# Statistics in a reading of their own, transposes and layer norm in one stage, variances of four chunks side by side

## The chip, the cores and the metric

The kernel runs on one NeuronCore of a Trainium2 chip. Its engines are TensorE (PE, with its weight loads PEld), VectorE (DVE), ScalarE (ACT), GpSimd (POOL) and SyncE (SP); they run from queues of their own and meet through semaphores. SP, ACT and POOL issue DMA transfers, which share 16 DMA engines. The metric is the device time of one execution in microseconds (us). The kernel before takes 5235.69 us, the median of three runs (5234.29 to 5239.15).

## The reference

An image `x` of 256 x 256 pixels and 128 channels goes through four residual layers, each behind a group normalisation `_gn` over 32 groups of 4 channels and all pixels. All is float32. Only the head of layer 0 is touched by the change:

```python
def _gn(v, G=32, eps=1e-5):
    g = v.reshape(B_, H_, W_, G, C_ // G)
    m = mean(g, axis=(1, 2, 4)); s = var(g, axis=(1, 2, 4))
    return ((g - m) / sqrt(s + eps)).reshape(v.shape)
# layer 0: z = _gn(x)
mu = mean(z, -1); var = mean(square(z - mu), -1)
zn = (z - mu) * rsqrt(var + EPS) * ln_scale + ln_bias   # layer norm over the channels
q, k, v, g = zn @ Wq, zn @ Wk, zn @ Wv, sigmoid(zn @ Wg) # four heads of 32
scores = q k^T / sqrt(32) + (zn @ Wb)                    # attention along rows, with a pair bias
x = x + ((g * softmax(scores) v) @ Wo)
```

Layer 1 is a recurrence in the frequency plane, whose small 7 x 7 kernels are Fourier transformed first (the "spectrum"); layer 2 is a triangle product, layer 3 a 3 x 3 convolution with a dense layer. Each takes `x` from the layer before.

## The kernel before, in words

The kernel keeps every image transposed in DRAM: channels on the 128 partitions, 65536 pixels along the free dimension (`xT`, `x1T` ..., `znT` for the normalised one). `run` (L1343) calls one function after another. What concerns us is what comes ahead of the attention loop.

*`attention_weights` (L218) and `bounded` (L380 and on)* load layer 0's weights over ACT's queue, scale them, and compute from small Gram matrices a bound on the scores, whose flag decides later which attention loop runs. `wv`, `wq` and so on are scaled on DVE (L237); `terms` takes one square root on ACT.

*`transpose_in` (L158)* goes over 64 blocks of 1024 pixels. SP loads a block `xin` (512 KB); PE transposes it in eight 128 x 128 pieces into `pt` (L202); DVE copies one half to `xo` and ACT the other (L208, L206), so that eight neighbouring pixels stand together; DVE takes two `bn_stats` per block (L211) for the group statistics; POOL stores `xT` (L212). There are five buffers of each tile and three of `pt`. Between blocks 12 and 57, sixteen calls of `spectrum` (L181) each do eight small matmuls `ph` and a copy to `H` on ACT (L188); after eight of them ACT gathers `H` into `HH` by four copies over 14 partitions (L192), and SP stores it to DRAM. The statistics are merged by `group_affine` (L75), with matmuls `pm`, `pv` over groups and a square root `sd` on ACT; `centering` (L122) makes a matrix `lc` that scales and subtracts the channel mean in one matmul, and a column `cb` (matmul `pc`).

*The first part of `attention` (L293 to L372)* goes over the same 64 blocks again. SP loads pairs of blocks back from `xT` (1 MB, L311). Per block: `centre`, two matmuls `zc` of 512 pixels; `squares`, ACT's square `sq` and DVE's copy with the column added, `zs`; `normalise`, two matmuls `var` of the squares with a matrix of 1/128, so that every partition holds the variance, ACT's Ln and Exp for the inverse root `rs`, DVE's product `zn`, and POOL's scale and bias (L336). Per pair, `pair_bias`: four matmuls `pbias` of 32 output rows, each in a column strip of its own, a copy `bi`, POOL's store of `znT` (L346) and four small stores of the bias by SP (L349). This part is written in program order on each engine (`keep_in_program_order`, L299); elsewhere a scheduler orders the instructions of each engine when the kernel is built. At the end the bias is loaded back (L288), and the attention loop begins with `ppq`.

Pools of tiles have a fixed number of buffers; a tile's producer waits until the tile that had the buffer is released. PSUM has eight banks of 512 float32 per partition.

## Time and profile before

| what | before |
|---|---|
| median of three runs | 5235.69 us |
| the profiled execution | 5238.88 us |
| its span on the chip | 5237.0 us |
| mean granted TensorE clock | 0.975 |
| PE, DVE, ACT, POOL busy | 4997.8, 4091.4, 3684.9, 344.4 us |
| transposing stage (to the last `pc`) | 0 to 227.3 us |
| layer norm stage (first `zc` to last `pbias`) | 227.5 to 493.8 us |
| DMA, whole span | 788.58 MB, mean 151 GB/s |

A line of a group reads: line of the kernel, engine, operation, output<-input by the program's names, shapes, count; then busy us and mean ns of one; then idle time of the engine ahead of these, and what ended it. One float32 matmul appears as two records, each of a weight load and a product. A line of a stretch gives its length, and the busy us of PE, weight loads, DVE, ACT, POOL with their instruction counts, then the granted clock (1.00 is full), the share of the DMA engines, and GB/s. A line of the timeline or of the chain gives the start in us and the duration, merged over neighbours. In waits, "a <- b: 65.9, 30, 11.8" means that a waited for b 65.9 us in 30 times, 11.8 at the longest.

### The profile page before, as it was taken

What the parts mean: (1) busy time and instruction counts of PE and PEld (TensorE: products, weight loads), DVE (VectorE), ACT (ScalarE), POOL (GpSimd) and SP (SyncE); (2) the same over time, 40 slices, a digit from 0 to 9 for tenths busy, and PEclk for the clock granted to TensorE, in tenths of its full rate; (3) what the DMA queues carried; (4) which work ended last, traced back from release to release, by engine and by line L of the source; (5) the groups of instructions that cost most, each with busy time, mean ns of one, the idle gap of its engine ahead of it and who ended that gap; (6) DMA issues with size and microseconds to landing.
All of it is one profiled execution on the core that took longest, in us unless ns stands there. A gap on an engine that the chain in (4) does not pass through costs nothing.

```text
span 5237.0 us, 75959 instructions
## 1 busy us (share of the span) xinstructions
PE 4997.8 (95%) x30067; PEld 2805.6 (54%) x30067; DVE 4091.4 (78%) x4886; ACT 3684.9 (70%) x5051; POOL 344.4 (7%) x552
## 2 busy tenths in 40 slices
PE   6699999999999899999999998999999989989999
PEld 4433555555555333333333333349999944339999
DVE  5665999999999799999999999554433446679886
ACT  4376888888888799999999998883333357762110
POOL 1132000000000000000000000000011000000000
PEclk7799999999999899999999999999999999999999
DMA  8875222222222122122222221767766678855432
GB/s 290 335 271 206 73 86 82 85 80 83 86 85 82 62 70 70 66 73 68 70 70 67 73 70 65 286 253 272 251 229 231 224 288 295 295 206 188 148 123 65
DMA packets 185921, 788.58 MB, mean 151 GB/s; under 512 B 36083, under 2 KB 39432, under 8 KB 136384
## 3 DMA queue, kind: packets, MB, share of 16 engines
q1 hardware_dynamic: 120212, 514.73, 29.2%
q0 software_dynamic: 60416, 268.46, 13.3%
q8 instruction: 240, 3.93, 0.3%
q10 hardware_dynamic: 4936, 0.50, 0.1%
q14 instruction: 117, 0.96, 0.1%
HBM read 512.28 MB, written 271.32 MB: 150 GB/s over the span
## 4 chain that ended last, share of the span: by engine, by line
issue 50%; PE 41%; DVE 5%; POOL 2%; DMA 1%; ACT 1%; POOLq 0%; ACTq 0%; DVEq 0%; SPq 0%
PE z L60 9%; PE m L60 7%; PE zc L60 4%; PE po L60 4%; PE nd L60 3%; PE sc L60 3%; PE var L60 2%; PE py L60 2%; DVE stats L966 1%; DVE x L966 1%; PE ppq L60 1%; PE ppv L60 1%; PE px L60 1%; PE ppk L60 1%; PE ppg L60 1%
## 5 line engine op out<-in xcount | busy, mean ns | idle before, releaser
L471 DVE TENSOR_TENSOR e<-sc,bT 128x1024 f32<-128x1024 f32 x512 | 602.9, 1219 | 52.0 <-PE sc L60 52.0
L54 ACT ACTIVATE e<-e 128x1024 f32<-128x1024 f32 x512 | 540.3, 1055 | 64.1 <-DVE e L471 54.9
L966 DVE TENSOR_TENSOR LR<-z,sg 128x512 f32<-128x512 f32 x256 | 268.3, 1049 | 365.6 <-ACT sg L54 358.6
L60 PE MATMUL m<-U,v 128*128 128x128 f32 x4608 | 516.6, 276 | 6.6 <-DVE v L1281 6.6
L60 PEld LDWEIGHTS m<-U,v 128*128 128x128 f32 x4608 | 516.4, 192 | 6.7 <-DVE v L1281 6.7
L60 PE MATMUL z<-wf,zt 128*128 128x128 f32 x4096 | 460.9, 276 | 4.3 <-DVE zn L966 3.6
L60 PEld LDWEIGHTS z<-wf,zt 128*128 128x128 f32 x4096 | 460.6, 193 | 5.5 <-DVE zn L966 4.4
L54 ACT ACTIVATE sg<-z 128x512 f32<-128x512 f32 x256 | 152.8, 597 | 308.7 <-PE z L60 306.8
L60 PE MATMUL var<-sq,omat 128*128 128x512 f32 x768 | 360.8, 599 | 1.2 <-ACT rs L54 1.2
L54 ACT ACTIVATE rs<-var,eps 128x1024 f32<-128x1024 f32 x192 | 213.2, 1111 | 169.7 <-PE var L60 169.7
L60 PE MATMUL sc<-tq,tk 32*128 32x256 f32 x4096 | 299.0, 403 | 2.3 <-DVE e L471 1.4
L471 DVE TENSOR_TENSOR ks<-e 128x1024 f32<-128x1024 f32 x256 | 300.6, 1215 | 0.0
L60 PEld LDWEIGHTS sc<-tq,tk 32*128 32x128 f32 x4096 | 187.6, 185 | 160.3 <-issue 97.1
L60 PE MATMUL nd<-e,tv 128*32 128x256 f32 x4096 | 271.8, 383 | 0.0
L60 PE MATMUL zc<-xin,lc 128*128 128x512 f32 x512 | 248.6, 609 | 6.0 <-DVE zn L966 5.5
L54 ACT ACTIVATE dn<-dn 128x512 f32<-128x512 f32 x384 | 241.6, 629 | 12.7 <-DVE dn L471 1.9
L60 PEld LDWEIGHTS var<-sq,omat 128*128 128x128 f32 x768 | 137.9, 189 | 203.8 <-issue 155.2
L60 PE MATMUL av<-y,ident 128*128 128x512 f32 x384 | 192.2, 609 | 44.0 <-DVE y L803 44.0
L60 PE MATMUL po<-LR 128*128 128x256 f32 x1024 | 222.2, 380 | 6.9 <-DVE LR L966 6.9
L1318 ACT COPY m4s<-m 128x512 f32<-128x512 f32 x32 | 18.7, 585 | 286.8 <-PE m L60 286.8
L60 PEld LDWEIGHTS po<-LR 128*128 128x128 f32 x1024 | 194.1, 190 | 34.2 <-DVE LR L966 7.7
L54 ACT ACTIVATE rs<-rs 128x1024 f32<-128x1024 f32 x192 | 202.9, 1057 | 6.1
(325 smaller groups left out, 10085.5 us busy)
## 6 DMA issues: line engine op xcount, KB each, us to landing
zt<-znT SPq DMA_DIRECT2D x128, 1024.0 KB
znT<-zn POOLq DMA_DIRECT2D x64, 1024.0 KB, 4.7
xin<-x2T SPq DMA_DIRECT2D x64, 1024.0 KB
xr<-x3T SPq DMA_DIRECT2D x46, 768.0 KB
xin<-in_x_dram SPq DMA_DIRECT2D x64, 512.0 KB
xT<-xo POOLq DMA_DIRECT2D x64, 512.0 KB, 10.5
xr<-xT SPq DMA_DIRECT2D x64, 512.0 KB
xin<-xT SPq DMA_DIRECT2D x32, 1024.0 KB
```

Source lines behind the costliest of these rows:

```text
L54: return self.nc.scalar.activation(out, in_, func, bias=bias, scale=scale, **kw)
L60: return self.nc.tensor.matmul(out, lhsT, rhs, start=start, stop=stop)
L471: pin = lambda f: lambda *a, **k: tc.keep_in_program_order(f(*a, **k))
L966: pin = lambda f: lambda *a, **k: tc.keep_in_program_order(f(*a, **k))
L1318: nc.scalar.copy(m4, m[4])
```

## The change

The statistics get a reading of `x` of their own, and the transposes move into the layer norm stage.

- `statistics` replaces `transpose_in`. It reads `x` untransposed in 32 tiles `xin` of 2048 pixels (pixels on partitions), subtracts the first pixel from all (`sh`, `xs` on DVE), squares on ACT (`sqx`), and lets PE sum both over the partitions into one PSUM bank, `acc`: four column strips of 32 rows, two for the sums and two for the squares. Four matmuls with `sel` and a few DVE operations turn it into mean and variance per channel. Three tiles stay in SBUF (`kept`), so the next stage need not load them. The statistics no longer come from `bn_stats`.
- The spectrum moves with it (`kernel_rows`). `HH` is gathered in two halves, the first by ACT, the second by POOL, and stored in four pieces rather than two. `attention_weights` becomes a generator: loads first, its arithmetic at tile 23 of the program; the built order of each engine spreads both between the tiles.
- The layer norm stage goes over 32 pairs of blocks. Each round does `turn` for the next pair (16 transposes, four half copies, one `xT` store of 1 MB by POOL, one load of `xin` by SP two pairs ahead), then `variance`, one `centre`, `normalise`, `pair_bias` of the pair before, and the other `centre`. `zc` now reads `xo` in SBUF; `xT` is not read here.
- The variances of the four chunks of a pair go to four column strips of one PSUM bank (`var`, 32 rows each), so Ln and Exp run once over 512 columns rather than twice over 1024. Four row-strip matmuls with `spread` (32 rows by 128 columns of 1/32) then spread the inverse roots over all partitions, `pr`, and DVE's product reads `pr` from PSUM.
- PSUM in this stage: three buffers of two banks shared by `pt`, `zc`, `pr`, and two of one bank shared by `var` and `pbias`. The weights of the later layers are loaded in the layer norm stage; before, their loads stood among the first transposes.

```diff
+    def kernel_rows(self, sp, ps, HD_):
...
+        def spectrum(g):
+            n, g0 = divmod(2 * g, CG)
+            ph = ps.tile([P, 2, N], F32, name="ph", bufs=2)
...
+            nc.scalar.copy(H[n][:, :, g0:g0 + 2].rearrange("q u c -> q c u"), ph)
+            if g0 + 2 == CG:
+                for h in range(2):
+                    o = slice(64 * n + 32 * h, 64 * n + 32 * h + 2 * KS)
+                    u = slice(h * N // 2, (h + 1) * N // 2)
+                    for k in range(4):
+                        copy = nc.gpsimd.tensor_copy if h else nc.scalar.copy
+                        copy(HH[o, :, CG * k:CG * (k + 1)], H[n][32 * k:32 * k + 2 * KS, u])
+                    nc.sync.dma_start(HD_[n][:, u], HH[o])
+    def statistics(self, wp, weights, HD_, kept, src):
...
+            io = c.enter_context(self.pool(name="p0", bufs=2))
...
+            acc = ps.tile([P, 512], F32, name="acc")
+            order = list(range(KEPT, NM)) + list(range(KEPT))
+            for n, m in enumerate(order):
+                if m < KEPT:
+                    xin = kept[m]
+                else:
+                    xin = io.tile([P, 2, 1024], F32, name="xin", bufs=3)
+                nc.sync.dma_start(xin, src(m))
+                for b in range(2):
+                    xs = io.tile([P, 1024], F32, name="xs")
+                    V.tensor_tensor(xs.rearrange("p (t c) -> p t c", t=8), xin[:, b].rearrange("p (t c) -> p t c", t=8),
+                                    sh.unsqueeze(1).to_broadcast([P, 8, P]), ALU.subtract)
+                    sq = io.tile([P, 1024], F32, name="sqx")
+                    self.act(sq, xs, AF.Square)
+                    for j, t in enumerate((xs, sq)):
+                        for h in range(2):
+                            o = 64 * j + 32 * h
+                            self.mm(acc[o:o + 32], ones[:, :32], t[:, h * 512:(h + 1) * 512],
+                                    start=n == 0 and b == 0, stop=n == NM - 1 and b == 1)
+                if n == 2:
+                    spectrum = self.kernel_rows(sp, ps, HD_)
+                    next(weights)
+                elif 5 <= n < 21:
+                    spectrum(n - 5)
+                elif n == 23:
+                    weights = next(weights)
...
-                def normalise(b):
-                    var = ps.tile([P, 2, 512], F32, name="var", bufs=1)
-                    for k in range(2):
-                        mm(var[:, k], self.omat, sq[b][:, k * 512:(k + 1) * 512])
...
+            wide = lambda name: ps.tile([P, 1024], F32, name=name, tag="w")
+            row = lambda name: ps.tile([P, 512], F32, name=name, tag="r", bufs=2)
+            def turn(m):
+                load(m + 2)
+                xo[m] = io.tile([P, 2, P, 8], F32, name="xo")
+                for b in range(2):
+                    pt = wide("pt").rearrange("c (t p) -> c t p", t=8)
+                    for t in range(8):
+                        transpose(pt[:, t], xin[m][:, b, t * P:(t + 1) * P], self.ident)
+                    for h, f in enumerate((acopy, copy)):
+                        f(xo[m][:, b, :, 4 * h:4 * h + 4], pt[:, 4 * h:4 * h + 4].rearrange("c t p -> c p t"))
+                nc.gpsimd.dma_start(xT[:, m * 2048:(m + 1) * 2048], xo[m].rearrange("c b p t -> c (b p t)"))
...
+            def variance(m):
+                var = row("var")
+                for k in range(4):
+                    mm(var[32 * k:32 * k + 32], m32, sq[m, k // 2][:, (k % 2) * 512:(k % 2 + 1) * 512])
+                rs[m] = work.tile([P, 512], F32, name="rs")
+                act(rs[m], var, AF.Ln, bias=self.eps)
+                act(rs[m], rs[m], AF.Exp, scale=-0.5)
+            def normalise(m):
+                zn[m] = io.tile([P, 2048], F32, name="zn")
+                pr = [wide("pr") for _ in range(2)]
+                for k in range(4):
+                    mm(pr[k // 2][:, (k % 2) * 512:(k % 2 + 1) * 512], spread[32 * k:32 * k + 32], rs[m][32 * k:32 * k + 32])
+                for b in range(2):
+                    z = zn[m][:, b * 1024:(b + 1) * 1024]
+                    tt(z, zs[m, b], pr[b], ALU.mult)
                     nc.gpsimd.tensor_scalar(z, z, lns, lnb, ALU.mult, ALU.add)
...
+            turn(0)
+            centre(0, 0)
+            centre(0, 1)
+            for m in range(NM):
+                turn(m + 1)
+                variance(m)
+                centre(m + 1, 0)
+                normalise(m)
+                pair_bias(m - 1)
+                centre(m + 1, 1)
```

## The prediction

> **What bounds the kernel now.** I read the busy time by stretches first, then the rate of the DMA engines, the waits, and the chain that ended last. In the stretches (length, then busy us of PE, weight loads, DVE, ACT, POOL, then granted clock, DMA share, GB/s) two stages lie before the attention loop:
>
> ```profile
> 100.00:150.00 50.00, 27.97 (x156) 23.65 (x147) 28.82 (x48) 26.10 (x23) 8.56 (x17) 0.67 0.85 332
> 150.00:200.00 50.00, 27.64 (x138) 23.86 (x136) 30.55 (x50) 9.37 (x16) 9.01 (x17) 0.61 1.01 367
> 300.00:350.00 50.00, 50.00 (x155) 18.88 (x153) 33.20 (x32) 39.68 (x39) 18.88 (x20) 1.00 0.70 270
> 600.00:650.00 50.00, 50.00 (x523) 26.43 (x519) 46.19 (x54) 43.39 (x64) 1.60 (x3) 1.00 0.30 96
> ```
>
> Up to 227 us (transposes) no compute engine is near full and DMA is. From 227 to 494 us (layer norm) PE is full at full clock and DMA has 30% to spare. From 494 us on is attention, where PE is full again. The transposing stage in finer steps (GB/s of 40 steps between 120 and 215 us), and its waits (total us, times, longest):
>
> ```profile
> GB/s 254 376 350 369 386 421 417 417 423 416 423 411 417 421 423 417 419 669 159 78 105 205 404 367 378 385 378 400 409 416 419 416 417 419 414 421 426 424 428 426
> ```
> ```profile
> PEld pt L202 <- ACT xo L206: 65.9, 30, 11.8
> DVE xo L208 <- DMA xT<-xo: 46.2, 19, 10.9
> ```
>
> The plateau is about 420 GB/s, with a hole near 163 us where ACT copies HH (before that, four such copies held ACT from 103.3 to 117.8). So stage one is 64 MB at 420 GB/s, 160 us, and some 65 us of start, holes and tail. In the layer norm the chain returns to the same instruction every 8.06 us (start, duration):
>
> ```profile
> 374.42 1.91 PE var L60 x4
> 382.48 1.92 PE var L60 x4
> 390.54 1.91 PE var L60 x4
> ```
>
> 8.06 us is one pair of blocks, 2048 pixels, and PE has no gap in it: stage two is 32 x 8.06 = 258 us and 8 of ends.
>
> **What the Trainium skill says.** "TensorE: Matmul & The Clock Gate", Part 3: small matmuls in different 32-row or 32-column strips run at once, four row strips at N=512 measured 3.07 times faster. The trace agrees: pbias, four matmuls in column strips, takes 1.06 us below, against 4 x 0.86. The same page, Part 1 and Part 4: an idle PE falls to half clock, and transposes do not count as busy in the same way. Agrees: 0.61 to 0.67 in the transposing stage, 1.00 in the layer norm. "HBM Reference", Specifications: a core streaming alone gets about 425 GB/s; here 417 to 428. "SBUF — State Buffer", Who interferes with whom: a DVE instruction with two SBUF inputs and a GpSimd one that reads SBUF exclude each other. No row before shows such a collision.
>
> **The change, part by part.** Prices, from groups (busy us, mean ns) and, last, from the timeline (start, duration):
>
> ```profile
> L208 DVE COPY xo<-pt 128x512 f32<-128x512 f32 x64 | 43.0, 683 | 51.6 <-DMA xT<-xo 46.2 <-PE pt L202 4.8
> L206 ACT COPY xo<-pt 128x512 f32<-128x512 f32 x64 | 36.7, 588 | 108.9 <-DVE xo L208 96.8 <-DMA ev<-in_c_cols_dram 12.0
> L192 ACT COPY HH<-H 14x4096 f32<-14x4096 f32 x8 | 28.8, 3604 | 0.2
> L188 ACT COPY H<-ph 128x512 f32<-128x512 f32 x16 | 16.2, 1034 | 17.1 <-PE ph L60 17.1
> ```
> ```profile
> 402.07 1.88 PE L60 MATMUL var<-sq,omat 128*128 128x512 f32 x4
> 405.60 1.06 PE L60 MATMUL pbias<-zn,wb 128*32 128x512 f32 x8
> 504.88 1.91 PE L600 MATMUL pbt<-ident,bias 128*128 128x128 f32 x16
> 602.99 1.15 PE L60 MATMUL sc<-tq,tk 32*128 32x256 f32 x16
> ```
>
> *Removed:* the 32 MB reading of xT back, the bn_stats (78.5 us of DVE), stage one as it stood. All of 0 to 227.3 us falls away, and stage two's 266.2 us (first zc 227.5, last pbias 493.8).
>
> *Stage S (statistics).* It reads 33.6 MB: 80 us at 420 GB/s, 1.25 us per half tile (1024 pixels, 64 of them). DVE: 64 subtractions at 1.22 (row zn<-zs,rs) = 78 us, and some 45 small operations of the bound at about 0.22 = 10. ACT: 64 squares at 1.06 (row e<-e, 1055 ns, the same shape between SBUF tiles) = 68. H copies 16 x 1.03 = 16.5, HH copies 8 at half of 3.6 = 14.4, table loads and seven late DMA issues (0.45 each) = 6: 105 us. PE: per half tile four matmuls in four column strips, 0.9 to 1.1 us at full clock when the two pairs overlap as pbias does, 1.75 when they do not or the clock is half. 58 to 112, and the spectrum matmuls 15 (24.6 at the old clock).
>
> No engine alone sets S; the order in the built program does. The spectra and HH copies stand among the first 24 squares. ACT up to there: 24 x 1.06 + 16.5 + 14.4 + 1.5 + 3.2 = 61 us. Xs and its squares have two buffers each, so while ACT does six H and four HH copies in a row (13.4 us), DVE stands still and then, after three tiles (7.5 us), so do SP's loads. I add 6 us of waits: DVE's wv stands in front of the subtractions and waits for rawv, which ACT now loads only after its sixth square (a load takes some 4 us, as at the start of the old stage), and PE's queue holds spectra between the sums. The other 40 half tiles run at the DVE's and DMA's 1.25: 50 us. The first square starts at about 12.3 (row load, its broadcast, first subtraction; the old first transpose was at 16.8). The tail is acc 1.75 cold, its copy 0.7, the sums over partitions 3, and the old chain pm to pc 3.3 (224.0 to 227.3): 9. Together 12.3 + 61 + 6 + 50 + 9 = 138.
>
> Not shown before: HH's eight copies on POOL. Nearest row: its 2048-element memset, 1.79 us. Less than nothing is excluded, as the half that they take off ACT is already counted. Bounds: 0 if DVE stands still then anyway, 8 x 2.2 = 18 if each one locks the subtractions out (both inputs lie in SBUF); I take 4, as half of them fall into ACT's burst. S ends at 142, bounds 118 to 165.
>
> SP's own queue: the four HD stores wait there on POOL and ACT in front of the next tile loads. Hidden while three tiles are in hand; that is the same stall, not counted twice. Two store instructions more, 0.4 us each.
>
> *Stage B (transposes and layer norm), PE per 2048 pixels:* 16 transposes 1.91 (row pbt, same form at full clock), four zc 3.44 (as now: two take 1.72), var in column strips 1.1, pr in row strips 1.1 (row sc: 16 records of 256 columns, 1.15 overlapping the next, next start 1.08 later), pbias 1.1: 8.65. Switching between strip forms costs about 0.05 each; today pbias adds 1.18 to 6.88. I take 8.8, bounds 8.4 and 9.6.
>
> Who else: ACT 2 x 0.59 + 2 x 1.10 + 0.60 + 0.63 = 4.6 (6.5 now); DVE 2 x 0.68 + 2 x 1.28 + 2 x 1.22 + 0.68 = 7.0; POOL 2 x 1.19 + two issues 1.1 = 3.5; DMA 3.18 MB at 420 GB/s = 7.6. PE sets the pace, the cover of DMA is 1.2 us. Chains: PE queues var after 1.9 us of transposes, which covers the last square (1.1); zc (1.72) covers Ln and Exp (1.3 with handing over); xo's copies end about 0.7 before zc needs them, since DVE first finishes zs. The three wide PSUM buffers return in that order without a wait. If these covers fail, each costs its overlap, some 0.5 per round, 16 us.
>
> Ends: first transposes cold 3.6, two blocks' zc cold 6.5 (227.54 to 234.00 now), 31 rounds x 8.8 = 273, then var, Ln, Exp, pr, two products, POOL's pass: 7.5 to the last pbias. 290.6 against 266.2: +24.
>
> *Moved, at nothing:* the late weights (1.2 MB, 3 us of DMA) lie beside the first rounds, whose first three tiles are kept in SBUF and need no load; without that cover 3 us. The xT store moves behind the zn passes on POOL, which is idle 60% of a round. From the last normalise on, each engine's order is the same as before, so attention and all after cost what they cost.
>
> *Sum:* (142 - 227.3) + 24 = -61 to -62. Against the profiled execution's own 5238.88 us (span 5237.0 and 1.9 around it) that is 5177; that execution lies 3.2 us above the median of the runs, 5235.69, so 5174.
>
> **Rivals.**
> 1. *S runs at the DMA's pace* (H and HH copies fully hidden): 12 + 80 + 17 of waits and tail = S ends near 118, 5150. For it: nothing but ACT stands over 90 us. Against: two buffers only.
> 2. *S is bound by cold PE*: 64 x 1.75 + 29 = 141, in part overlapped, S ends near 165, 5197. For it: clock 0.61 to 0.67 in the old stage one at 55% busy. Against: a full PE earns the clock (1.00 in the layer norm).
> 3. *B loses the clock, the slower side.* Transposes and waits of a tiled stage leave PE at half clock part of each round. The saving is gone when a round takes 8.8 + 62/31 = 10.8 us, a mean clock of 0.81; at 0.75 a round is 11.7, 5264. For it: transposes ran at 0.6 before. Against: they are 1.9 of 8.8 us, the rest is dense.
> 4. *Side by side is not side by side:* var and pr serial, 2 x 3.44 in place of 2.2, a round of 13.5, 5320. Against: pbias and sc have exactly these forms and overlap.
>
> **How the numbers follow.** Own forecast 0.52 (its range 5150 to 5197), rival 1 0.18, rival 2 0.16, rival 3 0.11, rival 4 and others 0.03. A measurement tells 0.2% (10.5 us) from no change. Of rival 3 half reaches slower, the other half stays within 0.2% or a little faster. Faster 0.87, same 0.05, slower 0.08. S from 118 to 165 crossed with rounds of 8.4 to 9.6 spans 5138 (118 and 8.4) to 5222; the range, 5138 to 5215, leaves out 1 in 10 on either side, rivals 3 and 4 being most of the upper one.
>
> **What would show it.** S: ACT at 85% or more up to about 80 us, a gap in DMA there, then about 400 GB/s; pc near 142. B: rounds of 8.8 us, PE full, clock 1.00, DMA near 0.85, var and pr about 1.1 us per four. PE idle before var, zc or pr in every round, or waits on xin, would prove me wrong in B; a clock below 0.8 or DVE held by POOL in S would move S.

## The result, and the profile after

The changed kernel takes 5220.91 us, the median of ten runs (5218.07 to 5227.12), against 5237.38 us of the kernel before in ten runs on the same chip (5234.29 to 5247.31). The ratio is 0.9968 with a 95% interval of 0.9958 to 0.9978: 16.5 us faster, where 62 had been forecast. The profiled execution took 5220.43 us, 18.4 less than the one of before (5238.88).

| stage, us | before | forecast | after |
|---|---|---|---|
| ahead of the layer norm: end of `pc` | 227.3 | 142 | 167.6 |
| from there to the start of the last `pbias` | 266.5 | 290.6 | 313.1 |
| start of the last `pbias` | 493.8 | 432.6 | 480.7 |
| all that follows, to the end of the span | 4743.2 | the same | 4737.9 |

So both new stages are too long, the statistics by 25.6 us and the layer norm by 22.5, and together they eat 48 of the 62. Only 13.1 us are gained by the last `pbias`. After it the engines do the same work. From the first `ppq` on, the profiled executions of all the kernels here take 4734.6 to 4741.8 us (4741.4 before, 4735.8 after), so the 5.3 us of the last row can't be told from such differences.

The stretches of the changed kernel, in the columns of before. The first lies wholly in the statistics, the second holds their end, the third lies in the layer norm stage, the fourth in attention:

```profile
100.00:150.00 50.00, 36.15 (x214) 7.59 (x216) 32.24 (x27) 33.50 (x31) 6.68 (x4) 0.84 0.82 279
150.00:200.00 50.00, 42.94 (x238) 19.45 (x230) 29.94 (x42) 26.35 (x32) 8.25 (x10) 0.93 0.65 239
300.00:350.00 50.00, 45.80 (x261) 20.66 (x263) 34.66 (x38) 24.73 (x33) 19.11 (x22) 1.00 0.94 327
600.00:650.00 50.00, 50.00 (x492) 26.71 (x491) 46.21 (x54) 43.04 (x63) 1.60 (x3) 1.00 0.28 86
```

In the first stretch no engine is near full, and DMA, which moved 332 GB/s in the same stretch before and 420 on its plateau, moves 279. In the layer norm PE was full before (50.00) and now has 4.2 us of holes in 50, at full clock. DMA stands at a share of 0.94 there with only 327 GB/s. The traffic as a whole hardly shrinks (785.52 MB against 788.58): the reading of `xT` is gone, but a second reading of `x` has taken its place.

The rate of the DMA engines in the changed kernel between 90 and 150 us, 40 steps of 1.5 us:

```profile
GB/s 303 390 410 344 46 0 41 235 412 11 0 0 0 33 396 320 344 401 401 483 115 328 79 87 139 355 421 380 309 320 412 251 235 412 309 421 410 415 415 412
```

A step counts the bytes of the packets that start in it. There are three holes. Two (96 to 101 us, 103.5 to 111) lie in and just behind ACT's gathering of `HH` (97.1 to 104.7), when SP's loads have no free tile. The third, from 120 to 127 us, is another thing: tiles are being loaded in it, but in most of its steps only 79 to 139 GB/s start. What the engines waited for up to 168 us (total, times, longest), and the copies of the spectrum in that window:

```profile
ACT L54 <- DMA ka<-in_L_conv_A_imag_dram: 16.0, 1, 16.0
PEld acc L60 <- ACT sqx L54: 60.7, 51, 7.5
DVE xs L232 <- DMA xin<-in_x_dram: 12.1, 6, 7.3
```
```profile
L195 POOL COPY HH<-H 14x2048 f32<-14x2048 f32 x8 | 18.9, 2362 | 83.6 <-ACT H L188 83.4
L188 ACT COPY H<-ph 128x512 f32<-128x512 f32 x16 | 15.6, 1018 | 11.9 <-PE ph L60 11.9
L195 ACT COPY HH<-H 14x2048 f32<-14x2048 f32 x8 | 15.2, 1896 | 0.2
```

PE mostly waits for ACT's squares, as forecast. But DVE's wait for a tile of `x` in the third hole was in no step of mine, nor was ACT's start. ACT's queue is busy issuing the `ka` loads until 16.04 us and loads a table then, and the first square starts at 17.34 (forecast 12.3).

One round of the layer norm on the chain of work that ended last (start, duration, what):

```profile
295.57 1.12 ACT sq L54
...
296.72 1.30 DVE zs L360
...
298.06 1.98 PE zc L60 x4
...
303.16 2.00 PE zc L60 x4
...
305.19 1.12 ACT sq L54
```

From one square to the same square of the next pair are 9.62 us (31 rounds of them, against 8.8 forecast and 8.06 before). The chain leaves PE twice in a round: for a square of ACT and then a `zs` of DVE, both of the same `zc`, and for the copies `xo`. The waits from 200 to 460 us say what PE misses, with 27 rounds in the window:

```profile
DVE zs L360 <- ACT sq L54: 80.8, 54, 2.6
PEld zc L60 <- DVE zs L360: 36.9, 27, 1.4
PEld zc L60 <- DVE xo L360: 34.8, 27, 1.3
```

And the records of a round in time (in brackets an engine's idle time and what ended it):

```profile
298.06 1.98 PE L60 MATMUL zc<-xo,lc 128*128 128x512 f32 x4 [0.46 <-DVE zs L360]
...
300.08 1.12 ACT L54 ACTIVATE sq<-zc,cb 128x1024 f32<-128x1024 f32 x1 [3.39 <-PE zc L60]
...
301.23 1.28 DVE L360 TENSOR_SCALAR zs<-zc,cb 128x1024 f32<-128x1024 f32 x1 [0.37 <-ACT sq L54]
...
301.72 1.06 PE L60 MATMUL var<-sq,mean 128*32 128x512 f32 x8
...
302.43 1.28 DVE L360 COPY xo<-pt 128x512 f32<-128x512 f32 x2
...
303.16 1.99 PE L60 MATMUL zc<-xo,lc 128*128 128x512 f32 x4 [0.38 <-DVE xo L360]
...
305.08 1.14 PE L60 MATMUL pr<-rs,spread 32*128 32x512 f32 x8
```

Variances and their spreading take 1.06 and 1.14 us per four, as forecast: side by side they are. PE's work in a round is 8.78 us, and 0.84 us of holes come to it. Each has the same beginning. `zs` starts when ACT's square of the same `zc` is over, in all 54 cases of the window, though neither needs the other's result. At 298.06 PE waits for such a `zs` to give a buffer back. At 303.16 it waits for DVE's part of `xo`, which stands behind a `zs` in DVE's queue, and that behind the square.

### The profile page after: what moved, and what is told of

It is laid out like the page before. It is cut to its first block, busy times and chain, and to the rows that moved or that the text cites. A ratio compares the mean times of both kernels' runs of the same rounds, so it can differ in the third digit from the quotient of the medians.

```text
span 5218.6 us, 77252 instructions
## 1 busy us (share of the span) xinstructions
PE 5007.7 (96%) x30845; PEld 2752.8 (53%) x30845; DVE 4091.5 (78%) x4827; ACT 3649.4 (70%) x5052; POOL 347.1 (7%) x528
## 2 busy tenths in 40 slices
DMA packets 184288, 785.52 MB, mean 151 GB/s; under 512 B 35184, under 2 KB 38534, under 8 KB 134718
## 4 chain that ended last, share of the span: by engine, by line
PE 56%; DVE 33%; issue 5%; ACT 4%; DMA 1%; ACTq 0%; POOL 0%; SPq 0%; POOLq 0%; DVEq 0%
PE z L60 9%; PE m L60 7%; PE nd L60 7%; PE zc L60 6%; PE sc L60 5%; PE po L60 4%; DVE tr L885 3%; DVE t L882 3%; DVE y L882 3%; DVE p L882 3%; DVE yf L882 3%; PE ppq L60 3%; PE ppv L60 2%; PE px L60 2%; PE ppk L60 2%
## 5 line engine op out<-in xcount | busy, mean ns | idle before, releaser
L60 PEld LDWEIGHTS sc<-tq,tk 32*128 32x128 f32 x4096 | 187.6, 185 | 160.4 <-issue 97.1
L54 ACT ACTIVATE rs<-var,eps 128x1024 f32<-128x1024 f32 (+1 forms) x160 | 164.1, 1026 | 131.6 <-PE var L60 131.6
L54 ACT ACTIVATE sq<-zc,cb 128x1024 f32<-128x1024 f32 x128 | 142.2, 1111 | 142.5 <-PE zc L60 141.9
L60 PE MATMUL var<-sq,omat 128*128 128x512 f32 x512 | 237.3, 596 | 1.2 <-ACT rs L54 1.2
L1045 DVE SCALAR_TENSOR_TENSOR ga<-py,twbo,ga 128x1024 f32<-128x1024 f32 x64 | 82.1, 1284 | 149.7 <-PE py L60 149.7
L60 PE MATMUL bx<-p,ident 128*128 128x512 f32 x384 | 192.3, 610 | 0.0
```

Of the source, the lines that this page charges most:

```text
L54: return self.nc.scalar.activation(out, in_, func, bias=bias, scale=scale, **kw)
L60: return self.nc.tensor.matmul(out, lhsT, rhs, start=start, stop=stop)
L1045: pin = lambda f: lambda *a, **k: tc.keep_in_program_order(f(*a, **k))
```

## The experiments

Each kernel was run beside the kernel before. Times are medians, the ratio is to the kernel before with its 95% interval, and "pc" is the start of the matmul that ends the statistics (167.1 in the changed kernel). The kernel before took 5236.2 to 5239.1 us beside them.

| kernel | us | ratio | pc |
|---|---|---|---|
| changed | 5220.91 | 0.9968 [0.9958, 0.9978] | 167.1 |
| `b_zsfirst` | 5205.37 | 0.9940 [0.9923, 0.9956] | 166.4 |
| `b_acopy` | 5210.34 | 0.9949 [0.9932, 0.9965] | 166.7 |
| `b_both` | 5192.14 | 0.9914 [0.9897, 0.9930] | 162.5 |
| `b_oldvar` | 5365.66 | 1.0245 [1.0225, 1.0266] | 169.1 |
| `v_alone` | 5228.63 | 0.9981 [0.9974, 0.9988] | 230.1 |
| `v_order` | 5198.52 | 0.9926 [0.9909, 0.9942] | 223.5 |
| `v_best` | 5183.45 | 0.9899 [0.9883, 0.9916] | 211.8 |
| `s_nospec` | 5158.23, one run | | 134.9 |
| `s_pin` | 5207.29 | 0.9937 [0.9920, 0.9953] | 180.0 |
| `s_pin_bufs` | 5204.01 | 0.9932 [0.9916, 0.9949] | 181.0 |
| `s_pin_hdq` | 5214.28 | 0.9952 [0.9935, 0.9969] | 191.0 |
| `s_spread` | 5199.51 | 0.9925 [0.9908, 0.9941] | 175.6 |
| `s_hand` | 5200.93 | 0.9931 [0.9914, 0.9947] | 176.0 |
| `s_hand_ld` | 5202.14 | 0.9930 [0.9913, 0.9947] | 179.7 |
| `s_hd2` | 5203.13 | 0.9939 [0.9922, 0.9955] | 174.3 |
| `s_late` | 5179.79 | 0.9888 [0.9872, 0.9905] | 146.9 |
| `b_late` | 5183.26 | 0.9898 [0.9882, 0.9915] | 156.6 |

### The layer norm: handing over between ACT and DVE, or DMA?

Two readings of the 9.62 us stood against each other. One: DVE reads `zc` only after ACT has, and PE waits for DVE, once directly and once for the copy behind it. The other: at a share of 0.94 DMA is the bound, and the waits only pass its pace on. Each hole of the first theory can be taken away by itself. `b_zsfirst` has DVE read block 0's `zc`, and ACT square the result in SBUF:

```diff
-                sq[m, b] = work.tile([P, 1024], F32, name="sq")
-                act(sq[m, b], zc, AF.Square, bias=cb)
-                zs[m, b] = work.tile([P, 1024], F32, name="zs")
+                sq[m, b], zs[m, b] = (work.tile([P, 1024], F32, name=n) for n in ("sq", "zs"))
+                if b: act(sq[m, b], zc, AF.Square, bias=cb)
                 ts(zs[m, b], zc, cb)
+                if not b: act(sq[m, b], zs[m, b], AF.Square)
```

> Every block 0 of the second stage: DVE reads zc first (zs), and ACT squares zs out of SBUF instead of reading zc too. Hand-over theory (ACT's and DVE's readings of one PSUM tile follow each other, so a zc buffer comes free 1.1 us late): the wait of the next zc on zs, 0.46 us in each round, goes; the round falls from 9.62 to about 9.16 us, 14 us in all, about 5207 us. DMA theory (the second stage runs at the pace of DMA, 0.95 busy at 338 GB/s): the round stays at 9.62, the time at 5221, and the wait turns up elsewhere.

`b_acopy` gives each block of transposes whole to one engine, so that nothing of block 0, which PE needs first, stands behind DVE's `zs`:

```diff
-                    for h, f in enumerate((acopy, copy)):
-                        f(xo[m][:, b, :, 4 * h:4 * h + 4], pt[:, 4 * h:4 * h + 4].rearrange("c t p -> c p t"))
+                    f = copy if b else acopy
+                    f(xo[m][:, b], pt.rearrange("c t p -> c p t"))
```

> ACT copies the whole first block's transposes out of PSUM, DVE the whole second block's, in place of a half of each tile by each engine. Hand-over theory: the wait of zc on xo, 0.38 us in each round, goes; round about 9.24 us, 12 us in all, about 5209 us. DMA theory: round 9.62, time 5221.

`b_both` has both edits.

> The two edits together. Hand-over theory: PE has no idle time left in a round, which falls to PE's own work, 8.78 us; 26 us in all, about 5195 us. DMA theory: round and time as they were (9.62, 5221). A mixture, a round of 9.1 to 9.4 with waits on loads or stores, would say that DMA is the next bound just behind.

They give 5205.37, 5210.34 and 5192.14 us. A round takes 9.09, 9.17 and 8.64 us, so the two waits add up: 0.53 and 0.45 alone, 0.98 together. The same stretch of `b_both`:

```profile
300.00:350.00 50.00, 50.00 (x286) 22.02 (x284) 37.53 (x36) 25.54 (x30) 20.00 (x24) 1.00 1.01 379
```

(As before: PE, weight loads, DVE, ACT, POOL, then clock, DMA share, GB/s.) PE is full again, and DMA moves 379 GB/s with the same bytes per round. In the changed kernel, then, a share of 0.94 was no bound: the share counts the time that packets take, and for the same bytes they took 8% more of it there (0.94 at 327 GB/s against 1.01 at 379). The hand-over theory holds, the DMA theory falls. The share is now 1.01, and the bytes of a round (3.18 MB) at 379 GB/s are 8.4 us: DMA stands right behind PE.

### The variances alone

If side-by-side variances are what the layer norm gains from, they can be had without moving the statistics. `v_alone` is the kernel before, with this part of the change only (squares from `zs` in SBUF, four buffers of each, and three wide PSUM buffers):

```diff
...
-                    if b % 2 == 1:
-                        pair_bias(b // 2 - 1)
-                    normalise(b)
...
+                for m in range(NB // 2):
+                    centre(2 * m + 2)
+                    squares(2 * m + 2)
+                    variance(m)
+                    centre(2 * m + 3)
+                    squares(2 * m + 3)
+                    normalise(m)
+                    pair_bias(m - 1)
...
```

> The kernel before with one part of the change alone: the variances of four chunks in column strips of one PSUM tile, and their spreading back over the partitions in row strips; zs is formed first and squared out of SBUF. First stage as it was. If side by side does what the change's profile suggests (var 1.06 and pr 1.14 us per four in place of 2 x 1.72 for full variances), a round of 2048 pixels is 2 x 1.72 + 1.06 + 1.14 + 1.06 = 6.7 to 6.9 us in place of 8.06: 31 x 1.2 = 37 us less than before, about 5200 us, which is also less than the whole change. If the gain of the whole change comes from the statistics' own reading instead, this one is within 5 us of before.

It takes 5228.63 us, some 28 more than expected: a round fell from 8.06 to 7.81 us only. ACT's row and PE's in its timeline show why:

```profile
301.54 1.06 ACT L54 ACTIVATE sq<-zs 128x1024 f32<-128x1024 f32 x1 [3.85 <-DVE zs L305]
302.50 0.67 ACT L54 ACTIVATE rs<-var,eps 128x512 f32<-128x512 f32 x1
303.88 1.14 PE L60 MATMUL pr<-rs,spread 32*128 32x512 f32 x8 [0.85 <-ACT rs L54]
```

`var` had ended at 301.1, but in ACT's queue a square of the next pair, waiting 3.85 us for its `zs`, stands in front of the Ln. `v_order` moves that square behind the Ln and Exp in program order:

```diff
                     centre(2 * m + 2)
-                    squares(2 * m + 2)
                     variance(m)
+                    squares(2 * m + 2)
```

> As v_alone (the kernel before with the variances side by side alone), with one edit: on ACT the square of the next block comes after Ln and Exp of the variance instead of before them. In v_alone a round took 7.81 us, of which PE was idle 1.1 us ahead of pr, waiting for rs, because ACT's queue held a square, which waits for DVE, in front of Ln. If that queue order is the cause, the round falls to PE's own work, 6.7 to 6.8 us, 31 x 1.0 = 31 us less than v_alone, about 5197 us. If DMA or DVE (5.6 us of work in a round) is what holds it, the round stays above 7.5 us and the time within 10 us of v_alone's 5229.

5198.52 us, as expected. A round takes 6.89 us with PE full (50.00 of 50) and DMA at a share of 0.83. So this part of the change, alone and in the right order, gives 39 us (by the ratio), more than twice what the whole change gives.

`b_oldvar` is the counter test: the changed kernel with two full `var` per pair and no `pr`.

```diff
-                var = row("var")
-                for k in range(4):
-                    mm(var[32 * k:32 * k + 32], m32, sq[m, k // 2][:, (k % 2) * 512:(k % 2 + 1) * 512])
...
+                for b in range(2):
+                    var = wide("var")
+                    for k in range(2):
+                        mm(var[:, k * 512:(k + 1) * 512], self.omat, sq[m, b][:, k * 512:(k + 1) * 512])
...
```

> The change without its second half: statistics and transposes as in the change, but each block's variance as a full matmul for all partitions, and no spreading (no pr). PE per round: 1.91 + 3.44 + 3.44 + 1.1 = 9.9 us and ACT 2 x 1.1 more. If side by side is worth what its rows say, a round takes 10.3 to 10.9 us against 9.62 in the change, 20 to 40 us more than 5221, that is slower than before; if the hand-over waits hide PE's extra work, the round stays at 9.6 to 9.9.

It missed by over 100 us: 5365.66, rounds of about 14 us (12.8 to 15.5). The full `var` has to share the three wide buffers with `pt` and `zc`, and PE is busy 39 us of 50: its `var` waits 35.9 us (from 240 to 440 us) for a `zs` of DVE, and `zs` 112.3 us for squares of ACT. It is no price of the variances. That the three wide buffers are too few for this form fits these waits; a kernel with more was not run.

### The statistics: what keeps them at 167 us

First, how much the spectra cost at all. `s_nospec` is `b_both` without `ph`, `H` and the copies to `HH`:

```diff
-                    self.mm(ph[32 * k:32 * k + 32, j], ka[n][:, CG * k + g0 + j, :], tu)
-            nc.scalar.copy(H[n][:, :, g0:g0 + 2].rearrange("q u c -> q c u"), ph)
...
-                        copy(HH[o, :, CG * k:CG * (k + 1)], H[n][32 * k:32 * k + 2 * KS, u])
```

> b_both without the spectra: no ph matmuls, no H and no HH copies; HD is stored, filled with zeros, where it was. This leaves out part of the computation and prices it. ACT loses 16.5 + 15 us in the statistics, PE some 24 us, POOL its eight copies. If the copies and their bursts cost the stage its time beyond 1.25 us per half tile, pc comes to 17 + 80 + 9 + up to 12 for the stores, that is 106 to 118, 45 to 55 us under 162.5. If PE or the loads set the stage in the first part too, pc stays above 135.

`pc` starts at 134.9, not at 106 to 118. Spectra and gathering cost 27.6 us beside `b_both`. What is left over the DMA's 80 us is not theirs; waits for `xin` stay, 17.7 us in all, the longest of 9.9 us.

All kernels of this part but the last are made on `b_both`. Was it the order that the build chose? `s_pin` fixes the statistics in program order on their engines; `s_pin_bufs` gives `xs` and `sqx` a third buffer besides; `s_pin_hdq` issues, on `s_pin`, the `HD` stores from ACT's and POOL's queues instead of SP's.

```diff
-                    V.tensor_tensor(xs.rearrange("p (t c) -> p t c", t=8), xin[:, b].rearrange("p (t c) -> p t c", t=8),
-                                    sh.unsqueeze(1).to_broadcast([P, 8, P]), ALU.subtract)
+                    pin(V.tensor_tensor(xs.rearrange("p (t c) -> p t c", t=8), xin[:, b].rearrange("p (t c) -> p t c", t=8),
+                                        sh.unsqueeze(1).to_broadcast([P, 8, P]), ALU.subtract))
...
-                    sq = io.tile([P, 1024], F32, name="sqx")
+                    sq = io.tile([P, 1024], F32, name="sqx", bufs=3)
...
-                    nc.sync.dma_start(HD_[n][:, u], HH[o])
+                    (nc.gpsimd if h else nc.scalar).dma_start(HD_[n][:, u], HH[o])
```

> b_both (5192 us, end of the statistics, pc, at 162.5) with the statistics' instructions held in the order in which the program states them: one H copy behind each pair of squares, four HH copies in a row, in place of the order that was chosen at build time (six H and four HH copies in a row on ACT with no square between). Order theory (the bursts on ACT starve the pair of xs and square buffers, and so DVE, PE and the loads): pc falls by 10 to 15 us to about 150, the time to about 5179. Rival (PE at a low clock, or the hole in the loads behind the HD stores, sets the stage): pc stays within 5 us of 162.5.

> s_pin with three buffers each of xs and of the squares instead of two. If two buffers are too few to bridge ACT's H and HH copies, 4 to 8 us less than s_pin; if the total work of ACT (99 us) or PE sets the stage, within 3 us.

> s_pin with the four stores of HD issued by the engines that made them (ACT and POOL), so that they no longer stand in SP's queue, and in its ring, among the tile loads. Hole theory (the 13 us gap in the loads near 120 us comes from the 14-partition stores ahead of them): the hole goes, 8 to 10 us less than s_pin. Rival (the stores hold the same DMA engines from any queue, or the hole is hidden behind ACT's burst): within 3 us of s_pin.

All three are slower in the statistics than `b_both`: 180.0, 181.0 and 191.0. In plain program order ACT's copy of `H` comes right behind the matmuls that it needs, and ACT stands there, 36.4 us in all up to 180 us. The built order was better than that (11.9 us in the changed kernel). A third buffer is no remedy. `s_pin_hdq` settles nothing, since without the stores the build moved the kept tiles and the later weights ahead of the last loads in SP's queue. The two stores that POOL issued took 11.2 and 11.9 us to land, since their packets started when those of ACT's, from another queue, ended (at 95.8 and 155.3 us); this fits the Trainium skill ("DMA: Bandwidth & Descriptors", Issuing engines are not separate DMA queues), by which all issuers end on the same 16 engines.

What a store does to the tiles behind it. `s_hd2` stores each `HD` piece twice:

```diff
-                    nc.sync.dma_start(HD_[n][:, u], HH[o])
+                    for _ in range(2):
+                        nc.sync.dma_start(HD_[n][:, u], HH[o])
```

> b_both with each of the four HD stores issued twice, nothing else moved: it doubles the suspected cost. Each store of 448 KB from 14 partitions keeps 14 of the engines for 4.4 to 5.1 us, whatever stands behind it, at some 95 GB/s. If both pairs of stores are exposed, pc rises by 2 x 9.5 = 19 us to 181; if the first pair is hidden behind ACT's burst of copies, by 9 to 10 us; if tile loads do not wait for these stores, by less than 3.

`pc` moves from 162.5 to 174.3, by 11.8 us. The longest wait of DVE for a tile grows from 8.2 to 18.5 us (waits of `s_hd2` up to 172 us):

```profile
DVE xs L233 <- DMA xin<-in_x_dram: 28.9, 10, 18.5
```

The orders of ACT, DVE and POOL are those of `b_both`, so this is the price of the four added stores. The second pair stands bare in both kernels. In the changed kernel this is the third hole. In the timeline SP issues two stores, then loads; on the chain a load of a tile takes 13.02 us, and DVE stands 7.3 us for it:

```profile
115.28 0.83 SPq L196 DMA_DIRECT2D HD<-HH  x2
117.27 22.62 SPq L229 DMA_DIRECT2D xin<-in_x_dram  x6
```
```profile
117.27 13.02 DMA xin<-in_x_dram
```
A store reads 14 partitions. In the records of the packets its 14, of 32 KB each, run at once. From first packet to last, the first two stores of the changed kernel moved 96 and 88 GB/s, the second two, side by side, 112. Some 16 packets are under way at any time; in the hole the stores' are 12 to 14 of these, and the loads have what is left. The packets' times are of three kinds, clearest in a store of `s_hand` at 140.34 us: twelve took 4.83 to 5.12 us and two 2.50 to 2.55; the shortest of all took 1.21. So it looks as if they pass in fours, or in twos, through something that carries 32 KB in 1.21 us, that is 27 GB/s. The Trainium skill has an explanation ("SBUF — State Buffer", Door 1: The DMA port swizzle): 14 partitions from 0 or from 32 on reach 4 of 16 ports, a quarter of 436 GB/s, an estimate of 109. The rate agrees, and so do the three kinds (14 partitions are three times four and two); that the ports are the cause no run here shows.

Can the store be quicker? `s_spread` gathers `HH` in four groups of 14 partitions, two of them on POOL:

```diff
-                for h in range(2):
-                    o = slice(64 * n + 32 * h, 64 * n + 32 * h + 2 * KS)
-                    u = slice(h * N // 2, (h + 1) * N // 2)
+                for h in range(4):
+                    o = slice(32 * h, 32 * h + 2 * KS)
+                    u = slice(h * N // 4, (h + 1) * N // 4)
```

> b_both with HD stored from four groups of 14 partitions (a quarter of the rows each) instead of two; bytes and copied elements as before. In all kernels so far the loads nearly stop when HD is stored: some 17 us in the kernel before (14 partitions with 64 KB each), 8 to 9 us in the change (two groups with 32 KB each), at 20 to 160 GB/s. Theory: a store from 14 partitions is carried by two DMA engines, at some 27 GB/s each, and the tile loads' shares on these engines wait behind it, from whatever queue. Then four groups halve the stop to about 4 us, twice, and pc falls from 162.5 by 4 to 8 us, the time from 5192 to about 5186. Rival (the stop comes from ACT's bursts of copies, which starve the buffers): pc within 3 us of 162.5.

No: the first stores ran one after another at 87 GB/s, and twice as many copies of half the size cost more: ACT 16 x 1.04 us where 8 x 1.90 stood, POOL 16 x 1.33 where 8 x 2.36 stood. `pc` came to 175.6. That is 13.1 us more, which the copies' 3.9 us don't explain. SP, which takes its queue in order, stood 20.7 us in front of stores whose copies were not done; in `b_both` it was 7.5.

`s_hand` sets the order by hand instead: ACT copies `H` one tile after its matmuls, and ACT and POOL make one copy to `HH` each per tile.

```diff
+            later = lambda t, f: todo.setdefault(g + 5 + t, []).append(f)
+            later(1, lambda: pin(nc.scalar.copy(H[n][:, :, g0:g0 + 2].rearrange("q u c -> q c u"), ph)))
...
+                        later(2 + k, lambda k=k, h=h, copy=copy: pin(copy(
+                            HH[o[h], :, CG * k:CG * (k + 1)], H[n][32 * k:32 * k + 2 * KS, u[h]])))
+                for h in range(2):
+                    later(6, lambda h=h: pin(nc.sync.dma_start(HD_[n][:, u[h]], HH[o[h]])))
```

> b_both with the statistics' instructions in an order written by hand: the ph matmuls of a group behind the sums of its tile as in s_pin, but its H copy one tile later, and the HH copies one per tile (ACT and POOL each one) over the four tiles after that, so that ACT never waits for a matmul that stands behind its own last square, and never makes two copies in a row more than once a tile. s_pin lost 17.5 us to that wait (ACT H on PE ph 36.4 us in all). If the H and HH copies cost only ACT's time when they are spread: 16 tiles at about 3.6 us (PE: two sums and a ph), 15 us for HH, 16 tiles at 2.5, start 17, tail 7, and up to 10 for the HD stores: pc 135 to 147, time about 5168 to 5178. If the stage is bound by something else (HD stores, PE's clock), pc stays at 155 or more.

Again wrong: 176.0. What is left stands bare, in the waits up to 172 us and in one stretch:

```profile
DVE xs L237 <- DMA xin<-in_x_dram: 34.1, 3, 16.2
```
```profile
100.00:110.00 10.00, 0.40 (x2) 0.18 (x4) 1.68 (x2) 0.36 (x1) 0.00 (x0) 0.50 0.66 219
```

All compute engines stand for these 10 us, behind stores issued from 92.6 on. Here too SP had stood in front of stores, 11.6 us in all, until ACT's copies were done. `s_hand_ld`, which moves the `ka` loads to POOL's queue besides to free ACT's start, missed too: 179.7 and 5202.14 us. Its first square came at 25.0, as the build now put the weights' arithmetic ahead of it.

```diff
-                nc.scalar.dma_start(k[p0:p0 + KS, :, q0:q0 + KS], src)
+                nc.gpsimd.dma_start(k[p0:p0 + KS, :, q0:q0 + KS], src)
```

> s_hand with the eight loads of the small kernels issued on POOL's queue instead of ACT's, where six of them hold the first square until 17.3 us. If ACT's queue is what delays the start, the first square comes at about 12 us and pc 4 to 6 us earlier than in s_hand; if the first tile's arrival or its broadcast delays it, within 2 us.

If the stores are the cause, they have to go behind the last tile load. `s_late` is `s_hand` with only this changed (and `HH` in a pool that lives on into the layer norm):

```diff
-                    later(6, lambda h=h: pin(nc.sync.dma_start(HD_[n][:, u[h]], HH[o[h]])))
+                    self.stores.append(lambda h=h: pin(nc.sync.dma_start(HD_[n][:, u[h]], HH[o[h]])))
...
+            for f in self.stores:
+                f()
```

> s_hand with the four HD stores issued behind the last tile load of the statistics, and HH in a pool that lives on through the second stage. In s_hand the copies no longer starve the loads, and the loads' two stops behind the stores (16 us each) are bare: DVE waited 34.1 us for tiles in all, pc 176.0. If the stores' place in SP's queue is the cause, these waits go and pc falls by 30 to 34 us, to 142 to 146, and the stores lie under the end of the statistics and the first three rounds, whose tiles are in SBUF: about 5168 us. If the stores only stop the DMA engines elsewhere, the first rounds wait instead, and the time stays above 5190.

`pc` goes from 176.0 to 146.9, and the stretch that stood still is at work; DVE's wait for `xin` in the whole of the statistics is 3.1 us:

```profile
100.00:110.00 10.00, 8.77 (x68) 1.80 (x60) 8.02 (x6) 7.43 (x8) 3.96 (x2) 1.00 0.75 267
```
```profile
DVE xs L238 <- DMA xin<-in_x_dram: 3.1, 1, 3.1
```

Shown, then: in that order the stores' place in SP's queue, with all that hangs on it, costs 29.1 us. That is not the packets' price alone. SP's standing in front of them went as well (11.6 us to 1.2), and the build moved 19 loads of later weights and constants out of the statistics' part of SP's queue. The time falls by 21.1 us to 5179.79, since 7.8 are given back in the layer norm (292.5 us from the end of `pc` to the end of the last `pbias`, against 284.7). The stores hardly caused that: their last packet ends at 151.4 us, and the rounds up to 222 us take 8.64 us each. The transposes wait twice for `xin`, 5.4 us in all, at 224.8 and 237.5 us, after SP has issued the moved loads (175 to 215 us), which are the likely cause. This is the lowest time of a complete kernel here, 0.9888 of the kernel before [0.9872, 0.9905].

`b_late` makes the same move in `b_both`, without the order by hand.

> b_both (the order that was chosen at build time) with the same move of the HD stores alone. With the stores out of the way the build chooses another order for the statistics too, with the H copies between the squares. Of b_both's stops the second is bare (11.8 us more when doubled), the first half hidden behind the burst of copies: 12 to 20 us less, pc 143 to 150, time 5172 to 5180. If ACT's bursts set the stage, within 5 us of 5192.

`pc` 156.6, only 5.9 less than `b_both`, and 5183.26 us. Only 8.2 us of DVE's waits in `b_both` lie behind stores, so there was not more to gain by this move; the first pair's stop falls into a time in which DVE stands for other things (17.4 us from 80 to 102 us: 10.8 for the bound's small operations on ACT and PE, 6.6 for a square). Its build order also differs from that of `b_both` in other places, so the 5.9 is not the stores' price alone.

Last, the same gathering for the kernel with the old stages: `v_best` is `v_order` with `HH` in four groups as in `s_spread`, half of the copies on POOL.

> v_order (the kernel before with the variances alone, 5198.5 us) with HD stored from four groups of 14 partitions with 16 KB each in place of one with 64 KB, and half of the HH copies on POOL. If the two-engine theory holds, the two stops in the transposing stage shrink from some 17 us to about 4 us, part of which falls into ACT's copying that stands there anyway: 12 to 24 us less, 5175 to 5187 us. If the stop comes from ACT's copies or from elsewhere, within 5 us of 5198.5.

5183.45 us, within what was expected, but in part by luck. The expectation rested on two DMA engines carrying a store, and a store has 14 packets under way. What else the edit does, ACT's copying of `HH` down from 28.8 to 16.7 us, is not separated from the stores' new form. The statistics' own reading is not needed for this time: `v_best` keeps the old `transpose_in` and comes within 4 us of `s_late`, whose interval overlaps its own.

## Why the prediction was wrong

**Direction and what was right.** It is faster, but by 16.5 us and not 62; the time lies above the range's upper end of 5215. Right were PE's work in a round (8.78 us for 8.8), var and pr side by side (1.06 and 1.14), full clock in the layer norm (1.00, against rivals 3 and 4), POOL and DVE in each other's way (4 us taken: 58 subtractions at 1280 ns where those beside no copy took 1224, 3.2 us), and attention costing what it cost.

**Stage B, "The three wide PSUM buffers return in that order without a wait" and "xo's copies end about 0.7 before zc needs them".** These two steps failed. The price of failure stood in the text ("some 0.5 per round, 16 us"), but was left out of the forecast, and it is larger: 0.84 us of holes per round in the trace, 0.98 when both are removed, 26 to 30 us in 31 rounds. No count of busy time has it. In this program ACT's square (1.11) and DVE's `zs` (1.28) of one `zc` do not run together, so the buffer comes free after their sum, and DVE's copies begin later by the square. The Trainium skill states this exclusion ("PSUM — Partial Sum Buffer", PSUM bank collisions raise a hardware error: two engines' accesses to the same 32 partitions of one bank have to be guarded, a read against a read too); it was in my sums for no step. The trace agrees (80.8 us of waits, 54 of 54). That of before had it too. `zs` began after the square of the same `zc` in all 64 blocks, but this cost little, since a `zn` of 1.22 us stood in DVE's queue meanwhile. And in the transposing stage ACT's half of a `pt` was copied after DVE's half in all 64 blocks. The L206 line of the prediction shows it: the 96.8 us that ACT sits idle for DVE's `xo` are 36 waits, and all of them end within 0.08 us of the end of DVE's half. (For part of that time DVE itself was waiting. The halves lie in two banks and both engines write one `xo`, so what orders them there is open.)

**Stage S, "SP's own queue: … that is the same stall, not counted twice".** This failed. SP's own standing was hidden in the changed kernel, as forecast: 7.5 us in front of the first pair, and DVE waited for no tile there. But the stores are a stall of their own: the packets of a pair are 12 to 14 of the 16 under way for some 8 us, the tiles queue behind them, and DVE stands 7.3 us behind the second pair. I had asked who waits at SP, and not what DMA does after SP has gone on. The trace of before had the case. I put its hole near 163 us down to ACT's copies of `HH`, but these were over at 117.8. What stands ahead of the hole is one store, whose packets of 64 KB start from 161.9 us on (the high steps) and end by 173.1, and beside them the rate falls for 8 us (timeline of before, then its rates from 158 us in 40 steps of 0.5):

```profile
153.74 0.48 SPq L193 DMA_DIRECT2D HD<-HH  x1
```
```profile
GB/s 418 418 426 426 410 418 418 672 1098 647 107 213 57 180 57 49 66 98 115 106 98 107 107 115 123 139 238 279 352 385 401 442 393 377 352 369 393 360 369 361
```

**"The first square starts at about 12.3"** was 17.34, 5 us late, behind the `ka` loads of ACT's queue. **"I add 6 us of waits"** and the "61" of ACT: the first part took 87.4 us (from 17.34 to the end of the last `HH` copy of ACT at 104.74) and not 67, with 28 squares in it and not 24. **"40 half tiles at 1.25: 50 us"** were 36 by then and took 56, with the 13.0 us load in it; the tail took 7 and not 9. The terms add up: 5 + 20.4 + 6 - 2, less about 4 for the collisions, whose 3.2 us lie inside the two parts, is the 25.6 of the table to rounding. With stores moved and copies spread, `s_late` ends at 147.5: the forecast's 142.3 plus the late start. So the sum of the work fits, and what was mis-sized are the waits.

**Rival 2** gave S an end of 165 and that is nearly the number that came, but hardly for its reason. In the same stretch the clock is 0.50 in `s_hand`, with PE at 0.40 of 10 us, and 1.00 in `s_late`, with PE at 8.77, so a low clock came where PE stood. It is not ruled out for a part: from 40 to 60 us PE was at work for 19.74 us of 20 at a clock of 0.83, and no run separates that. **Rival 1** adds up to 109 (12 + 80 + 17), not to the 118 that it names; both are far from what came.

**What stays open.** How the 25 us divide is settled only in part. Behind the stores DVE stands 7.3 us in the changed kernel, and their removal from the built order gives 5.9; the 29.1 us belong to the order by hand. The larger part, the 20.4 us up to the end of the copies, lies with the copies' order, PE and ACT, and no run divides it. In this part DVE also stood 10.7 us (3.5 and 7.2, between 85 and 96 us) in front of the bound's small operations, for ACT's `terms` and PE's `ptot`: a wait that is in no step of the forecast, and that no run takes away by itself. The late start was not mended by `s_hand_ld`. A single store that reads more than 14 partitions was not tried. Kernels with the same statistics differ by up to 4.6 us at `pc` (162.5 to 167.1 among the changed kernel, `b_zsfirst`, `b_acopy` and `b_both`), so differences of that size there say little.

## What to carry to other kernels

Where two engines read one PSUM tile, add their times up, and ask what waits for that buffer and what is queued behind the second reader; one of them can read the other's result in SBUF (with the copies regrouped, 28.8 us here). A DMA store from few partitions is charged to the loads that stand behind it, and the queue that issues it stands in front of it until its source is ready, so try it after the last of them. A part of a change that is priced by itself should be tried by itself: here the variances alone, in the right order on ACT, bring 39 us and the whole brings 16.5.

## What the runs showed of the hardware that was not expected

- A store from 14 partitions (448 KB) moved 88 to 112 GB/s, and the time of its packets grew with their size when 14 ran together: most of 64 KB took 8 to 10 us, of 32 KB up to 5.1, of 16 KB 2.2 to 2.5, while the shortest of 32 and 16 KB took 1.21 and 0.61. DVE stood 7.3 to 8.2 us for a tile behind a pair of them in the built order, and 18.5 with each store doubled.
- The share of the DMA engines did not tell what was left in them: 0.94 at 327 GB/s, 1.01 at 379 with the same bytes per round, and 0.66 in a stretch in which the compute engines stood (`s_hand`, 100 to 110 us).
- A copy of 14 x 2048 elements took 1.90 us on ACT and 2.36 on POOL; cut in two it took 1.04 and 1.33 per half (on POOL 1.03 in `v_best`).
- In these programs ACT and DVE never read one `zc` together: in 64 of 64 blocks before, and in 54 of 54 cases of the window after, the second began when the first was over.
- Transposes in the layer norm ran at a granted clock of 1.00 (16 in 1.91 us) between dense matmuls, where the old stage, with PE at work for 28 us of 50, had run them at 0.61 to 0.67.
